# A graph layer with gathers and one-hot products: more nodes by slots, fewer by chunks, a pause between gathers, and x theta^T computed beside B

## The chip, the core and the metric

The kernel runs on one core of a Trainium2 chip. The metric is the device time of one execution in microseconds; given is the median of ten runs.

## The reference

`x` is 6250 x 256; `src` and `dst` hold 100000 edges, sorted by `dst`. Cut to what matters:

```python
e = relu((x[dst] - x[src]) @ theta_w.T + theta_b + x[src] @ phi_w.T + phi_b)
out = segment_max(e, dst, num_segments=6250)
out = where(isfinite(out), out, 0.0)
return layernorm(x + out, axis=-1, eps=1e-5)
```

What depends on the destination is the same for all edges into a node, and relu doesn't change an order. So the kernel computes, for each node, `relu(max over its edges of B[src] + x theta^T)`, where `B = x (phi - theta)^T + biases` has one row for each source.

## The kernel before, in words

**B.** x is loaded in pieces of four rows per partition, transposed on TensorE (L669), copied by ACT (L671), multiplied by the weights (L675, two products of 128x256 for each 128 rows), and DVE adds the bias (L678). The pieces `b_sb` are stored to the tensor `b_rows` in HBM.

**Part 1, the chunks.** The first N1 = 6250 - 128*TILES nodes have the first edges of the sorted list. These edges are cut into 128 chunks of FIRST_STEPS columns, one chunk per partition. GpSimd gathers a column of 128 rows of `b_rows` by an indirect DMA (`gather`, L467 to 469), eight columns into one tile `g` of the pool `gathered` (RING tiles of 1 MB); DVE keeps the running maximum along the chunk, reset by `caps` at the border of a node (`run`, L717 to 726, the instruction at L722); SP writes the group to `maxima_1` in HBM. X_GROUPS of the even groups are gathered from x itself, before B is there, and multiplied on the chip (L696 to 699). `node_place` (L762), `places_1`, `chunk_heads`, `tails_1` (L811) and `heads_1` find the last edge of each node and carry a maximum over the borders of chunks.

**Part 2, the slots.** The last 128*TILES nodes lie TILES to a partition. From `dst_w`, a window of WINDOW edges per partition, ACT counts where each node's edges begin (L628, a sum of signs), eight counts in a batch; then a gather brings up to R = 36 sources of each node (`table_i`, L475). `sources` (L853 to 874) turns source numbers into a slot and a row; a slot is 375 rows of B, in KB = 3 blocks of 125. `choice` (L877) picks, two slots at a time, at most one edge of each node in each slot, and takes it out of what is left; `wanted` (L912) stores the choice to `chosen_rows`. `slot_part` (L939) brings the chosen rows of one slot for 1024 nodes, builds their one-hot (L949 on DVE, one block; L951 and L952 on ACT, two), multiplies it by the slot's rows of B in two terms (24 products, L959), and DVE keeps the maximum in `acc` (L970). With 17 slots and 4 chunks of nodes these are 68 parts. What wasn't chosen goes to a list (`list_pieces`, L980 to 1042) of LIST columns, gathered and reduced as part 1's chunks are (`group_2`, L1044), into `maxima_2`.

**End.** `rows_of` (L1051) loads x for a share of tiles, gathers their maxima, multiplies x by theta^T (L1071 to 1079), for part 2 transposes `acc` (L1086) and takes the larger, adds, and applies relu (L1087 to 1091). `normalise` (L1096) makes the layer norm on ACT and DVE (squares L1104, L1111) and stores the rows. The shares of part 1 lie among the list's groups, those of part 2 stand behind the last part.

**What sets the order.** Pieces are emitted as L1127 to 1177 say: `sources`; nine choice steps with two chunk groups behind each; the list's pieces; the remaining chunk groups with PACE slot parts per group; then the list's groups with PACE parts per group; what remains of the parts; the end. From that a scheduler makes one fixed order for each engine. Every engine takes its instructions in that order, an instruction that waits holds up all behind it.

Of the kernel before, what the change touches and what calls it, by code (L numbers as in the profile page):

```python
# [48 lines left out]
P = 128  # L49
# [3 lines left out]
RING = 7  # L53
GENERAL_STEPS = 17
FIRST_STEPS = 275
X_GROUPS = 5
X_BEFORE = 2
TILES = 32
LIST = 240
WINDOW = 640  # L60
# [5 lines left out]
PACE = 1.2  # L66
# [339 lines left out]
def gnn_kernel(ctx: ExitStack, tc: tile.TileContext, x, src, dst, theta_w, theta_b, phi_w, phi_b, out):  # L406
# [4 lines left out]
    Q = N // P  # L411
    LEFT = N - P * Q
    NT = Q + 1
    XQ = 4
# [8 lines left out]
    NB = N // ROWS  # L423
    NS = -(-NB // KB)
# [4 lines left out]
    assert D == 2 * P and LEFT > 0 and LEFT1 > 0 and Q % XQ == 0 and OWN % CW == 0  # L429
    assert (P - 1) * T + 1 < E <= P * T and N < ID_MASK and P * T <= EDGES and E + 8 * P <= EDGES  # L430
    assert N == NB * ROWS and SLOT * NS < ABSENT and KB * P <= SLOT and WINDOW <= 8 * P and P * T1 < E
    assert LIST % STEPS == 0 and TILES <= 32

# [4 lines left out]

    b_rows = dram.tile([N, D], FP, name="b_rows")
# [5 lines left out]

    x_main = x[: P * Q, :].rearrange("(p q) d -> p q d", q=Q)
    b_main = b_rows[: P * Q, :].rearrange("(p q) d -> p q d", q=Q)
    b_block = b_rows.rearrange("(b r) d -> r b d", r=ROWS)


    x_1 = x[: P * Q1, :].rearrange("(p q) d -> p q d", q=Q1)
    x_2 = x[N1:, :].rearrange("(p q) d -> p q d", q=TILES)
    out_1 = out[: P * Q1, :].rearrange("(p q) d -> p q d", q=Q1)
    out_2 = out[N1:, :].rearrange("(p q) d -> p q d", q=TILES)
    maxima_1t = maxima_1[: P * T1, :].rearrange("(p t) d -> p t d", t=T1)
    maxima_2t = maxima_2[: P * LIST, :].rearrange("(p t) d -> p t d", t=LIST)

    def iota(t, step, base, per_partition):
        nc.gpsimd.iota(
            t,  # L460
            pattern=[[step, t.shape[1]]],
            base=base,
            channel_multiplier=per_partition,
            allow_small_or_imprecise_dtypes=True,
        )

    def gather(to, table, offsets):  # L467
        nc.gpsimd.indirect_dma_start(  # L468
            out=to, out_offset=None, in_=table, in_offset=bass.IndirectOffsetOnAxis(ap=offsets, axis=0)
        )  # L470

    def gather_run(to, table, offsets):

        n = to.shape[1]
        nc.gpsimd.indirect_dma_start(  # L475
            out=to,
            out_offset=None,
            in_=flat(table, 0, [[n, EDGES // n], [1, n]]),
            in_offset=bass.IndirectOffsetOnAxis(ap=offsets, axis=1),
        )  # L480
# [15 lines left out]

    for i in of_x[:X_BEFORE]:
        gather_group(i, x)
# [28 lines left out]

    weights = const.tile([P, 2, KC, D], FP, name="weights")
    bias = const.tile([P, 1, D], FP, name="bias")

# [13 lines left out]
    with (  # L544
        tc.tile_pool(name="sort", bufs=1) as sort,
        tc.tile_pool(name="ps_sort", bufs=2, space=PSUM) as ps_sort,
    ):
        n_unsorted = nc.values_load(flags[0:1, 0:1])
        with tc.If(n_unsorted > 0):
            sort_edges(nc, sort, ps_sort, src, dst, src_list, dst_list, ident)  # L550
            load_chunks(nc.sync, dst_i, dst_list, T, EDGES)
            load_chunks(nc.sync, dst_1, dst_list, T1, EDGES)
            load_rows(nc.scalar, src_1, src_list, P * T1)
            for i in of_x[:X_BEFORE]:
                gather_group(i, x)
# [51 lines left out]
    accs = body.enter_context(tc.tile_pool(name="accs", bufs=1))  # L607
    acc = accs.tile([P, KC, OWN], FP, name="acc")
    index = body.enter_context(tc.tile_pool(name="index", bufs=1))
    dst_w = index.tile([P, WINDOW], I32, name="dst_w")  # L610
    gather_run(dst_w, dst_list, edge0_i)
    for i in of_x[X_BEFORE:]:
# [10 lines left out]
    BATCH = 8  # L623
    for j0 in range(0, TILES + 1, BATCH):
        j1 = min(j0 + BATCH, TILES + 1)
        for j in range(j0, j1):
            junk = index.tile([P, WINDOW], BF, name="junk")
            nc.scalar.activation(  # L628
                junk, local, AF.Sign, bias=halves[:, j : j + 1], scale=-1.0, accum_out=sums[:, j : j + 1]
            )  # L630
        nc.vector.tensor_scalar(begin[:, j0:j1], sums[:, j0:j1], 0.5, 0.5 * WINDOW, op0=ALU.mult, op1=ALU.add)
# [8 lines left out]

    with (
        tc.tile_pool(name="prep", bufs=1) as prep,
        tc.tile_pool(name="x_in", bufs=3) as x_in,
        tc.tile_pool(name="b_out", bufs=2) as b_out,
        tc.tile_pool(name="ps_t", bufs=3, space=PSUM) as ps_t,
        tc.tile_pool(name="ps_b", bufs=3, space=PSUM) as ps_b,
    ):
        w_in = prep.tile([P, 2, KC, D], FP, name="w_in")
        for i, w in enumerate((theta_w, phi_w)):
            nc.sync.dma_start(w_in[:, i], w.rearrange("(c p) k -> p c k", p=P))  # L650
        biases = prep.tile([P, 2, D], FP, name="biases")
        for i, b in enumerate((theta_b, phi_b)):
            nc.sync.dma_start(biases[:, i, :], flat(b, 0, [[0, P], [1, D]]))
        nc.vector.tensor_add(bias[:, 0, :], biases[:, 0, :], biases[:, 1, :])
        nc.vector.tensor_sub(w_in[:, 1], w_in[:, 1], w_in[:, 0])
        for i in (1, 0):
            for c in range(KC):
# [3 lines left out]
                nc.vector.tensor_copy(weights[:, i, :, c * P : (c + 1) * P], ps[:, 0])  # L661

        def b_of(to, rows):

            n = rows.shape[1]
            ps = ps_t.tile([P, 2, KC, P], FP, name="ps_xt")
            for i in range(n):
                for k in range(KC):
                    nc.tensor.transpose(ps[:, i, k, :], rows[:, i, k * P : (k + 1) * P], ident)  # L669
            x_t = prep.tile([P, 2, KC, P], FP, name="x_t", bufs=3)  # L670
            nc.scalar.copy(x_t[:, :n], ps[:, :n])  # L671
            ps = ps_b.tile([P, 2, D], FP, name="ps_b")
            for i in range(n):
                for k in range(KC):
                    nc.tensor.matmul(  # L675
                        ps[:, i, :], x_t[:, i, k, :], weights[:, 1, k, :], start=(k == 0), stop=(k == KC - 1)
                    )
            nc.vector.tensor_tensor(to, ps[:, :n, :], bias.to_broadcast([P, n, D]), op=ALU.add)  # L678

        for q in range(0, NT, XQ):  # L680
            n = min(XQ, NT - q)
            b_sb = b_out.tile([P, XQ, D], FP, name="b_sb")
            x_q = x_in.tile([P, XQ, D], FP, name="x_q")
            if q < Q:
                nc.sync.dma_start(x_q, x_main[:, q : q + XQ, :])
            else:
                nc.vector.memset(x_q[:, 0, :], 0.0)
                nc.sync.dma_start(x_q[:LEFT, 0, :], x[P * Q :, :])
            for i in range(0, n, 2):
                w = min(2, n - i)  # L690
                b_of(b_sb[:, i : i + w, :], x_q[:, i : i + w, :])
            if q < Q:
                nc.scalar.dma_start(b_main[:, q : q + XQ, :], b_sb)
            else:
                nc.scalar.dma_start(b_rows[P * Q :, :], b_sb[:LEFT, 0, :])
        for i in of_x:  # L696
            for k in range(0, STEPS, 2):
                rows = ring_tiles[i][:, k : k + 2, :]
                b_of(rows, rows)
# [14 lines left out]
    ps_fetch = fetch.enter_context(tc.tile_pool(name="ps_fetch", bufs=3, space=PSUM))  # L714
    last = {1: None, 2: None}
# [120 lines left out]

    def table(name, dtype=FP):
# [7 lines left out]
    BATCH_S = 2  # L845

# [6 lines left out]
    def sources():  # L853
        nc.vector.tensor_copy(source.rearrange(by_rank, r=R), table_i.rearrange("p j r -> p r j"))
        floor_of(work_1, source, ROWS)
        floor_of(work_2, work_1, KB)
        nc.vector.scalar_tensor_tensor(source, work_1, float(P - ROWS), source, op0=ALU.mult, op1=ALU.add)
        nc.vector.scalar_tensor_tensor(source, work_2, float(SLOT - KB * P), source, op0=ALU.mult, op1=ALU.add)
        nc.gpsimd.iota(
            rank.rearrange(by_rank, r=R),  # L860
            pattern=[[1, R], [0, TILES]],
            base=0,
            channel_multiplier=0,
            allow_small_or_imprecise_dtypes=True,
        )
# [6 lines left out]
        nc.vector.scalar_tensor_tensor(work_1, source, float(-ABSENT), work_2, op0=ALU.add, op1=ALU.mult)  # L872
        nc.vector.tensor_scalar(padded, work_1, float(ABSENT), None, op0=ALU.add)
        nc.vector.memset(unused, 1)


    def choice(s0):  # L877
# [17 lines left out]
        at = index.tile([P, BATCH_S, 1, TILES], I16, name="at")  # L895
        for i in range(n):
            blocks = min(KB, NB - (s0 + i) * KB)
            nc.vector.tensor_scalar(
                at[:, i, 0, :], low[:, i, :W], (blocks - 1) * P + ROWS, None, op0=ALU.min
            )  # L900
        nc.vector.tensor_copy(chosen[:, s0 : s0 + n, :], at[:, :n, 0, :])
# [24 lines left out]
    def slot_terms(s):  # L926

        blocks = min(KB, NB - s * KB)
        f = raw
        even = ROWS // 16 * 16  # L930
        nc.sync.dma_start(f[:even, :blocks, :], b_block[:even, s * KB : s * KB + blocks, :])
        nc.sync.dma_start(f[even:ROWS, :blocks, :], b_block[even:, s * KB : s * KB + blocks, :])
        terms = terms_of[s] = slots.tile([P, PARTS, KB, D], FR, name="terms")
        nc.scalar.copy(terms[:, 0, :blocks], f[:, :blocks])
        nc.vector.tensor_tensor(
            terms[:, 1, :blocks], f[:, :blocks], terms[:, 0, :blocks].bitcast(FP), op=ALU.subtract
        )

    def slot_part(s, c):  # L939
        if c == 0:  # L940
            slot_terms(s)
        blocks = min(KB, NB - s * KB)
# [4 lines left out]
        for b in range(blocks):  # L947
# [5 lines left out]
        for h in range(KC):  # L953
            ps = ps_fetch.tile([P, CW], FP, name="ps_f")
            n = blocks * PARTS
# [23 lines left out]

# [246 lines left out]
```

## Time and profile before

| | |
|---|---|
| median of 10 runs | 907.36 us (902.37 to 912.56) |
| the profiled execution | 914.0 us |
| its span in the trace | 912.2 us |
| mean granted TensorE clock | 0.854 |
| first gather of the tables (POOL) | 63.76 us |
| last gather of the tables ends | 104.0 us |
| first gather from `b_rows` | 123.94 us |
| last running maximum of the list ends | 830.7 us |
| first gather of the end | 836.6 us |

PE is TensorE's products, PEld its weight loads, DVE VectorE, ACT ScalarE, POOL GpSimd, SP the engine that issues most loads and stores. In a line of the costliest groups stand the line of the kernel, the engine, the operation, what it writes and reads with the shape, and how often; behind the first bar the busy time and the mean in ns; behind the second the engine's idle time just before these instructions, and what ended most of it. In a timeline line stand the start, the duration, and in brackets the idle time before it. "Issue" as a releaser is time in which an engine waited for nothing that the profile shows. The slices cut the span in 40 equal pieces, with the busy share in tenths.

### The profile page before, as it was taken

What the parts mean: (1) busy time and instruction counts of PE and PEld (TensorE: products, weight loads), DVE (VectorE), ACT (ScalarE), POOL (GpSimd) and SP (SyncE); (2) the same over time, 40 slices, a digit from 0 to 9 for tenths busy, and PEclk for the clock granted to TensorE, in tenths of its full rate; (3) what the DMA queues carried; (4) which work ended last, traced back from release to release, by engine and by line L of the source; (5) the groups of instructions that cost most, each with busy time, mean ns of one, the idle gap of its engine ahead of it and who ended that gap; (6) DMA issues with size and microseconds to landing.
All of it is one profiled execution on the core that took longest, in us unless ns stands there. A gap on an engine that the chain in (4) does not pass through costs nothing. (4 is left out here: it accounts for less than half of the span.)

```text
span 912.2 us, 9291 instructions
## 1 busy us (share of the span) xinstructions
PE 610.9 (67%) x2557; PEld 483.6 (53%) x2557; DVE 632.7 (69%) x1309; ACT 429.0 (47%) x680; POOL 652.8 (72%) x622
## 2 busy tenths in 40 slices
PE   0459799576402655979406795857979898874782
PEld 0248688465301544768304574646868677653661
DVE  2223599999978776778309784846979787793764
ACT  0159232557201333467603555355967757420575
POOL 6767457788888877777777477777777777774730
PEclk9979899878755777889856899878999999898897
DMA  7366346776644657777537798666888788867342
GB/s 250 111 191 220 118 162 205 252 255 218 224 143 143 207 182 246 234 234 265 169 104 241 262 295 272 208 193 230 277 279 268 236 279 256 282 220 276 101 160 108
DMA packets 63082, 195.61 MB, mean 214 GB/s; under 512 B 14071, under 2 KB 22795, under 8 KB 53515
## 3 DMA queue, kind: packets, MB, share of 16 engines
q1 hardware_dynamic: 32207, 112.01, 34.2%
q0 software_dynamic: 28272, 75.14, 28.4%
q10 hardware_dynamic: 2540, 7.75, 2.4%
q8 instruction: 23, 0.38, 0.2%
q14 instruction: 40, 0.33, 0.1%
HBM read 114.27 MB, written 81.38 MB: 214 GB/s over the span
## 5 line engine op out<-in xcount | busy, mean ns | idle before, releaser
L959 PE MATMUL ps_f<-hot,terms 128*128 128x512 f32 x1600 | 417.2, 421 | 175.8 <-DVE hot L949 127.7
L959 PEld LDWEIGHTS ps_f<-hot,terms 128*128 128x128 f32 x1600 | 322.3, 205 | 260.6 <-issue 124.7
L722 DVE SCALAR_TENSOR_TENSOR g<-g,caps 128x256 f32<-128x256 f32 x513 | 246.3, 482 | 147.3 <-DMA g<-b_rows,list_src 100.7
L468 POOL DMA_INDIRECT g<-b_rows,src x235 | 280.7, 1194 | 75.3 <-issue 65.9
L468 POOL DMA_INDIRECT g<-b_rows,list_src x240 | 246.3, 1026 | 73.1 <-issue 63.7
L951 ACT ACTIVATE hot<-want,minus_row 128x1024 fp32r<-128x1024 f16 x132 | 146.0, 1144 | 165.1 <-PE ps_f L959 145.8
L970 DVE TENSOR_TENSOR acc<-acc,ps_f 128x1024 f32<-128x1024 f32 x128 | 155.6, 1216 | 4.7 <-PE ps_f L959 4.3
L952 ACT ACTIVATE hot<-hot 128x1024 fp32r<-128x1024 f32 x132 | 133.8, 1049 | 0.4
L675 PE MATMUL ps_b<-weights,x_t 128*128 128x256 f32 x356 | 86.7, 400 | 20.7 <-ACT x_t L671 19.9
L675 PEld LDWEIGHTS ps_b<-weights,x_t 128*128 128x128 f32 x356 | 69.0, 199 | 34.3 <-ACT x_t L671 25.0
L468 POOL DMA_INDIRECT g<-maxima,place x49 | 47.7, 973 | 41.2 <-issue 20.8
L949 DVE TENSOR_SCALAR hot<-want,row_id 128x1024 fp32r<-128x1024 f16 x68 | 51.9, 763 | 2.2 <-ACT hot L952 1.2
L468 POOL DMA_INDIRECT g<-in_x_dram,src x40 | 38.7, 967 | 15.9 <-issue 11.3
L671 ACT COPY x_t<-ps_xt 128x512 f32<-128x512 f32 (+1 forms) x45 | 24.7, 577 | 50.8 <-PE ps_xt L669 31.3
L1077 PE MATMUL ps_e<-weights,x_t 128*128 128x256 f32 x128 | 34.9, 418 | 18.9 <-ACT x_t L1073 18.9
L475 POOL DMA_INDIRECT table_i<-src_list,begin_i x32 | 30.2, 944 | 13.9 <-issue 8.8
L1077 PEld LDWEIGHTS ps_e<-weights,x_t 128*128 128x128 f32 x128 | 24.5, 202 | 26.4 <-ACT x_t L1073 23.4
L771 ACT ACTIVATE junk<-ps,upper 128x275 bf16<-128x275 f32 x34 | 16.2, 482 | 45.4 <-PE ps L768 45.3
L678 DVE TENSOR_TENSOR b_sb<-ps_b,bias 128x512 f32<-128x512 f32 (+1 forms) x25 | 16.9, 679 | 26.5 <-PE ps_b L675 26.5
L628 ACT ACTIVATE junk<-local,halves 128x640 bf16<-128x640 f32 x33 | 27.4, 830 | 16.4 <-DVE local L615 13.2
L1077 PE MATMUL ps<-weights,x_t 128*128 128x256 f32 x68 | 20.5, 453 | 18.8 <-ACT x_t L1073 13.6
L1104 ACT ACTIVATE squares<-g,r 128x256 bf16<-128x256 f32 x49 | 24.3, 498 | 14.4 <-DVE r L1101 12.5
(194 smaller groups left out, 489.3 us busy)
## 6 DMA issues: line engine op xcount, KB each, us to landing
maxima<-g SPq DMA_DIRECT2D x64, 1024.0 KB
want<-chosen_rows SPq DMA_DIRECT2D x68, 256.0 KB
x_q<-in_x_dram SPq DMA_DIRECT2D x12, 512.0 KB
b_rows<-b_sb ACTq DMA_DIRECT2D x12, 512.0 KB
raw<-b_rows SPq DMA_DIRECT2D x16, 336.0 KB
g<-in_x_dram SPq DMA_DIRECT2D x5, 1024.0 KB
out_dram<-g SPq DMA_DIRECT2D x5, 1024.0 KB
g<-b_rows,list_src POOLq DMA_INDIRECT x240, 4.5
```

The lines of the kernel that those rows point to most:

```text
L468: nc.gpsimd.indirect_dma_start(out=to, out_offset=None, in_=table, in_offset=bass.IndirectOffsetOnAxis(ap=offsets, axis=0))
L475: nc.gpsimd.indirect_dma_start(out=to, out_offset=None, in_=flat(table, 0, [[n, EDGES // n], [1, n]]), in_offset=bass.IndirectOffsetOnAxis ...
L628: nc.scalar.activation(junk, local, AF.Sign, bias=halves[:, j : j + 1], scale=-1.0, accum_out=sums[:, j : j + 1])
L671: nc.scalar.copy(x_t[:, :n], ps[:, :n])
L675: nc.tensor.matmul(ps[:, i, :], x_t[:, i, k, :], weights[:, 1, k, :], start=(k == 0), stop=(k == KC - 1))
L722: nc.vector.scalar_tensor_tensor(g[:, k, :], last[part], caps[:, t : t + 1], g[:, k, :], op0=ALU.min, op1=ALU.max)
L949: nc.vector.tensor_scalar(hot[:, b, :], want, row_id[:, b : b + 1], None, op0=ALU.is_equal)
L951: nc.scalar.activation(hot[:, b, :], want, AF.Abs, bias=minus_row[:, b : b + 1], scale=1.0)
L952: nc.scalar.activation(hot[:, b, :], hot[:, b, :].bitcast(FP), AF.Relu, bias=1.0, scale=-1.0)
L959: nc.tensor.matmul(ps[:, w : w + 512], terms[:, part, b, h * P : (h + 1) * P], hot[:, b, w : w + 512], start=(i == 0), stop=(i == n - 1),)
L970: nc.vector.tensor_tensor(to, to, ps, op=ALU.max)
L1077: nc.tensor.matmul(a[:, i, :], x_t[:, 2 * i + c, :], weights[:, 0, c, :], start=(c == 0), stop=(c == KC - 1))
```

## The change

- TILES goes from 32 to 40, so part 2 has 5120 nodes instead of 4096, part 1 1130 instead of 2154; FIRST_STEPS goes from 275 to 146, LIST from 240 to 288, WINDOW from 640 to 800, PACE from 1.2 to 2.2. There are five chunks of nodes, so 85 parts.
- Three groups instead of five are gathered from x, eight gathers ahead of the branch, eight behind it and eight behind `dst_w`.
- The ring has four tiles; a second pool `ring_2` of seven, opened where the tables of the choice are closed, serves the list and the end.
- Every indirect gather is followed by an iota into a tile `pause` of 128x144, which nothing reads; fixed dependencies put gather, iota, gather in one order.
- x theta^T is computed with B (one product 512 wide for each half of x's columns), copied by ACT to `a_sb`, stored to `a_rows` in HBM, and loaded in `rows_of`; the end has no transposes of x and no products.
- Counts come in batches of ten, six by ACT and four by DVE.
- A slot's rows are dealt to its blocks in turn (row KB*p + b instead of blocks of 125); `sources` changes with it.
- One chunk group instead of two behind each choice step, a slot part behind every other one; parts are then paced by the list alone.
- The shares of the end have eight tiles each, and max and add are done on four tiles at once instead of two.

```diff
-RING = 7
-FIRST_STEPS = 275
-X_GROUPS = 5
-TILES = 32
-LIST = 240
-WINDOW = 640
-PACE = 1.2
+RING = 4
+RING_2 = 7
+FIRST_STEPS = 146
+X_GROUPS = 3
+TILES = 40
+LIST = 288
+WINDOW = 800
+PACE = 2.2
+PAUSE = 144
...
+    def indirect(out, in_, in_offset):
+        in_turn = mybir.DependencyInfo(mybir.DependencyClass.NoSync, mybir.DependencyReason.DATA)
+        one = nc.gpsimd.indirect_dma_start(out=out, out_offset=None, in_=in_, in_offset=in_offset)
+        if after_gather[0] is not None:
+            tc.add_manual_dep(one.ins, after_gather[0], in_turn, reason="a break between gathers")
+        count = iota(pause, 1, 0, 0)
+        tc.add_manual_dep(count.ins, one.ins.name, in_turn, reason="a break between gathers")
+        after_gather[0] = count.ins.name
...
-    for i in of_x[:X_BEFORE]:
-        gather_group(i, x)
+    gather_group(of_x[0], x)
...
-    BATCH = 8
+    BATCH, BY_SIGNS = 10, 6
...
+            else:
+                nc.vector.tensor_scalar(
+                    junk, local, halves[:, j : j + 1], None, op0=ALU.is_le, op1=ALU.add, accum_out=begin[:, j : j + 1]
+                )
...
+        weights = prep.tile([P, KC, 2, D], FP, name="weights")
...
+        for share in shares(4):
...
+            for i in range(0, n, 2):
+                w = min(2, n - i)
+                x_t = x_transposed(x_q[:, i : i + w, :])
+                ps = ps_b.tile([P, 2, 2, D], FP, name="ps_b")
+                for h in range(w):
+                    for k in range(KC):
+                        nc.tensor.matmul(
+                            ps[:, h], x_t[:, h, k, :], weights[:, k], start=(k == 0), stop=(k == KC - 1)
+                        )
+                add_bias(b_sb[:, i : i + w, :], ps[:, :w, 0, :])
+                nc.scalar.copy(a_sb[:, i : i + w, :], ps[:, :w, 1, :])
+            nc.scalar.dma_start(node_rows(b_rows, *share), present(b_sb, *share))
+            nc.scalar.dma_start(node_rows(a_rows, *share), present(a_sb, *share))
...
     def group_2(t0):
-        g = gathered.tile([P, STEPS, D], FP, name="g")
+        g = ring_2.tile([P, STEPS, D], FP, name="g")
...
+        x_f = ring_2.tile([P, STEPS, D], FP, name="g")
+        a = ring_2.tile([P, STEPS, D], FP, name="g")
...
+        nc.sync.dma_start(present(x_f, *share), node_rows(x, *share))
+        nc.sync.dma_start(present(a, *share), node_rows(a_rows, *share))
+        m = ring_2.tile([P, STEPS, D], FP, name="g")
...
-        for k in range(0, n, 2):
-            w = min(2, n - k)
-            ps = ps_tile().rearrange("p (i n) -> p i n", i=4)
-            for i in range(w):
-                for c in range(KC):
-                    nc.tensor.transpose(ps[:, 2 * i + c, :], x_f[:, k + i, c * P : (c + 1) * P], ident)
...
+        for k in range(0, n, 4):
+            w = min(4, n - k)
+            some = m[:, k : k + w, :]
...
-            nc.vector.tensor_tensor(two, two, a[:, :w, :], op=ALU.add)
+            nc.vector.tensor_tensor(some, some, a[:, k : k + w, :], op=ALU.add)
...
     sources()
     for s0 in range(0, NS, BATCH_S):
         choice(s0)
         wanted(s0)
-        for _ in range(2):
-            group_1(groups_1.pop(0))
-        if s0 == 0:
+        some_groups_1(1)
+        if s0 % 4 == 0:
             fetch_parts(1)
...
+    tables.close()
+    ring_2 = body.enter_context(tc.tile_pool(name="ring_2", bufs=RING_2, side="right"))
+    some_groups_1(len(groups_1))
...
+    for t0 in range(0, LIST, STEPS):
+        group_2(t0)
         pace += PACE
         while pace >= 1.0:
             fetch_parts(1)
             pace -= 1.0
```

## The prediction

> **What bounds the kernel now.** I read the busy shares first, then the slices, the costliest groups, the waits, and last GpSimd's own timeline.
>
> ```profile
> PE 610.9 (67%) x2557; PEld 483.6 (53%) x2557; DVE 632.7 (69%) x1309; ACT 429.0 (47%) x680; POOL 652.8 (72%) x622
> POOL 6767457788888877777777477777777777774730
> L959 PE MATMUL ps_f<-hot,terms 128*128 128x512 f32 x1600 | 417.2, 421 | 175.8 <-DVE hot L949 127.7
> L722 DVE SCALAR_TENSOR_TENSOR g<-g,caps 128x256 f32<-128x256 f32 x513 | 246.3, 482 | 147.3 <-DMA g<-b_rows,list_src 100.7
> L468 POOL DMA_INDIRECT g<-b_rows,src x235 | 280.7, 1194 | 75.3 <-issue 65.9
> L468 POOL DMA_INDIRECT g<-b_rows,list_src x240 | 246.3, 1026 | 73.1 <-issue 63.7
> ```
>
> No engine is full, but POOL's slices never fall below 4 until the last two, and the idle time in front of its gathers is "issue": it waits for nothing. The waits say so outright:
>
> ```profile
> POOL g L468 <- issue: 161.6, 492, 8.3
> ```
>
> and its timeline shows what the "issue" is:
>
> ```profile
> 57.70 0.95 POOL L468 DMA_INDIRECT g<-in_x_dram,src  x1 [0.30 <-issue]
> 58.65 1.29 POOL L859 IOTA rank<- 128x1152 f32 x1
> ...
> 103.10 0.94 POOL L475 DMA_INDIRECT table_i<-src_list,begin_i  x1 [0.30 <-issue]
> 104.04 0.36 POOL L459 IOTA local<- 128x240 f32 x1
> ```
>
> A gather has 0.30 ahead of it wherever gathers follow each other; so the undisturbed period is 0.946+0.305=1.25 us. The 599 gathers average 1.079+0.305. From 124 us (first gather from b_rows) to 828 us (end of the list) POOL does little else, so **POOL's gathers are the bound**; after 837 the end is a chain through POOL, DVE, ACT and the store. Gathers without a DVE operation beside them take 0.95; those beside a busy DVE 1.2 to 1.4 on the mean between 124 and 350 us, one of them 4.29 (at 263.9).
>
> **The change, part by part.** Counts after it are from the static order of each engine. All sums are against the profiled execution (span 912.2, time 914.0); this is 6.6 above the median 907.36.
>
> *Tables.* x gathers 40→24, table gathers 32→40. Gather dst_w stood behind 17 x gathers issued after the branch (27.50) and began at 48.84; 8 in front of it now, 9x1.25 less: 37.5, which edge0 (ready at 36.5) allows. From it to the first table gather lay 14.9 (63.76-48.84), with eight sign counts at 0.83 in it; six counts at 0.83x800/640 come out near the same, 12 to 13 since the first batch waits for fewer. So the first table gather comes at 49.5 and the last ends 40x1.252=50 later: 99.5 (before 104.0). The table lands at 101 (before 105.47).
>
> *B, and x theta^T beside it.* This is the loss that I am surest of. Before, 19 of the 25 bias adds (L678) came ahead of the first source operation, which waits for the table; the last, at 118.5, let the gathers start at 123.94. After, PE's product is 512 wide instead of 256, ACT copies the other half, and only 6 adds stand ahead of that wait; the other 19 lie among the source and choice operations, the last one behind the ninth choice step. So DVE must do all this after 101: the sources, 10.6 us before without the adds, times 40/32 nodes and 12 passes for 10, 15.6; 8.5 choice steps at 5.1 (start to start) times 40/32=6.3, 54; 19 adds at 0.6, 11.4; in all 81. PE's 17 to 19 pairs beside it need about 4.1 each (eight 512-wide products at twice the 0.227 us of a 256-wide one, and four transposes), 70 to 78: covered, but barely; without this cover nothing more is lost, since the longer of the two counts. With 5 us for store and start (123.94-118.54), b_rows is ready at **187**, 63 later than before. ACT's copies hide (3.60 busy in 19 us between 105 and 124).
>
> *Chunks.* 235 gathers from b_rows become 122. Two periods bound theirs: 1.25 undisturbed, 1.2 to 1.4+0.3=1.5 to 1.7 beside the choice. The choice is over by then, the list's making is not: 1.40, near to the 350-to-470 stage (120/92=1.30). 122x1.40=171. The ring falls from 7 to 4 tiles, three of which hold x groups, so groups 3 and 5 wait for groups 0 and 2 to be written behind the choice: 17 us. End of the chunks 187+171+17=375 (before 471: 96 us won back and more).
>
> *List.* 240 gathers become 288, with 9 of maxima and 2 for heads and scatter between: 299 periods of 1.315 (what 1.01 to 1.02+0.30 makes): 393, to 768; the last running max 2.5 later, 770.5 (before 830.7).
>
> *The pauses.* After each gather an iota of 128x144 is put in fixed order, so all 461 gathers on this path (40+122+299) carry one. No row shows an iota and a gather both unblocked. Bounds: the iota starts at the gather's end (58.65, 104.04) and could run in the 0.305 that is empty anyway: 0. Or it is added in full: between a 128x128 at 0.21 to 0.25 and a 128x240 at 0.36, so 0.25x461=+115. Below nothing: a break could at most take away the stretch by DVE, 0.15x122+0.063x299=-37. I take 0: the rows nearest to it show that an iota starts with no gap, that a gather starts 0.27 after what releases it, so that the 0.30 looks like the gather's own start, which the queue can do beside an iota.
>
> *Slots.* 68 parts become 85, 24 products each: 2040x0.235=480 us of PE (24x0.235=5.64 at granted clock 0.97, up to 6.26 lower). DVE gets 17x3.4 and ACT 17x4.4 us more, both under PE. In DVE's order 12 parts' one-hots and 27 of the 160 acc operations still stand behind the list's last running max; before, acc was done 7 us ahead of it. That **tail** has no gathers left to lie beside: 12.5 parts at 5.7 to 5.8, 72 us. What POOL wins at the list is paid here. acc done at 843.
>
> *End.* No x transposes, no theta products (128 at 418 ns there), but a load of x theta^T per share on SP, under the gathers of maxima. Five shares of eight: DVE 2x1.22 (max), 2x1.22 (add), 8x0.48, about 2.5 for the root: 11.2 each, 56; behind the last, ACT's 8x(0.50+0.5) and the store, 15; waits for ring tiles in shares 3 to 5, 4: **75** (before 81.5 behind the last running max). Span 918.
>
> A page of the Trainium skill speaks against the iotas. "SBUF — State Buffer", section "Who interferes with whom", says that DVE and GpSimd share one port pair by an exclusive lock and that the loser waits for the whole instruction; the trace agrees with its sense (0.95 alone, 4.29 at worst), though our stretch also stands beside running maxima with two SBUF inputs, which the page leaves out for descriptor writing. By it, an iota would be one more holder of the lock, 0.25 us at a time, and the sum would move up by as much as some 100 us if every one met DVE. "Perfetto Trace Analysis", section "GPSIMD Engine Instruction", says to time that engine by start-to-start spacing; by that rule the 0.30 may be part of the gather itself, with nothing to hide in, and the sum would be that of the first rival. I keep zero.
>
> **Sum.** 101+86+188+393+2.5+72+75 = 918 of span, 920 for such an execution, less 6.6: **913 us**, +0.6%. Its own range, with ±15 on the b_rows start, ±12 on the chunk period and ±10 on the end, is 885 to 940.
>
> **Rivals.**
> A. *The iota is additive.* For it: POOL is strictly in order, and the 0.30 may be fixed after each instruction. 0.21x461=+97: 1010; half hidden, 960. Decides from 0.05 us visible on.
> B. *Faster: the breaks and the quiet start take away the stretch.* Gathers fall to 0.946 everywhere, 37 us less, and with POOL idle during the choice DVE's steps shorten by some 8: 913-45=868; half of it 890. For it: undisturbed stages at 0.95; against it: in the list the stretch is only 0.063, and nothing says that an iota keeps DVE off a gather. It decides from 0.02 us per gather on.
> C. *The change doesn't shorten the chunks as it says*: the 122 gathers meet the list's making and the one-hots of the early parts at 1.6 instead of 1.40: +24, 937. For it: the mean of 200 to 350 us.
>
> **How the numbers follow.** My case 0.45, A 0.20, B 0.25, C 0.10. About 0.3% (2.7 us) is what a measurement can tell from no change. Of my case three tenths lie faster and an eighth within: faster 0.25+0.135=0.38, same 0.08, slower 0.54. The range takes all of B and my case, C, and A up to nine tenths of the iota visible: 866 to 1000.
>
> **What would show it.** First gather from b_rows near 187 (wrong, if near 130); spacing of list gathers 1.31 (A: 1.52; B: 1.25); last list running max near 770; PE busy without a break for 72 us behind it; 75 us from last acc to the end. If that tail is short, the sum is 30 to 60 too high; if the spacing is over 1.4, it is too low.

## The result, and the profile after

The changed kernel takes 1026.7 us in the median (1022.85 to 1032.59, nine runs), the kernel before 908.0 beside it: a ratio of 1.1313, 95% interval 1.1285 to 1.1341. That is 119 us slower, beyond the upper end of the forecast's range. The profiled execution's span is 1025.2. Here and below a ratio and its interval take only the executions within 1.5% of the fastest of their kernel (where one alone is left, no interval is given), a median takes all of them.

From the page of the changed kernel, the busy shares, the slices of POOL and the groups that answer to those shown before:

```profile
PE 671.1 (65%) x2607; PEld 497.0 (48%) x2607; DVE 688.5 (67%) x1233; ACT 488.2 (48%) x690; POOL 722.9 (71%) x1073
...
POOL 6688300178988888888888888888888886710560
...
L992 PE MATMUL ps_f<-hot,terms 128*128 128x512 f32 x2040 | 510.8, 411 | 136.8 <-DVE hot L982 114.9
...
L479 POOL DMA_INDIRECT g<-b_rows,list_src x288 | 298.8, 1038 | 47.8 <-issue 45.8
L750 DVE SCALAR_TENSOR_TENSOR g<-g,caps 128x256 f32<-128x256 f32 x432 | 205.9, 481 | 146.2 <-DMA g<-b_rows,list_src 103.5
...
L479 POOL DMA_INDIRECT g<-b_rows,src x122 | 151.4, 1241 | 104.2 <-DMA b_rows<-b_sb 76.3
...
L465 POOL IOTA pause<- 128x144 f32 x524 | 151.0, 288 | 3.4
```

Three things are new. POOL has a hole in slices 5 to 8 (from 107 to 202 us), and the group of chunk gathers names what ended it: 76.3 us on the store of B. What makes the store late is DVE's order: from the first source operation at 109.0 to the last bias add at 198.7 DVE was nearly always busy, and its 19 adds in that stretch waited 1.1 us for PE in all. Of DVE's groups from 109 to 199:

```profile
L693 DVE TENSOR_TENSOR b_sb<-ps_b,bias 128x512 f32<-128x512 f32 x19 | 13.0, 684 | 1.1 <-PE ps_b L709 1.1
```

Behind the hole POOL is fuller than before, but 151 us of its work are iotas, which bring nothing. And in slices 36 and 37 POOL has another hole. It lies beside this piece of the chain that ended last (start, duration, what):

```profile
868.08 72.60 PE ps_f L992 x312
```

72.6 us of products without a break, behind the end of the list. The timeline of GpSimd shows what a gather and its iota cost:

```profile
52.16 0.95 POOL L479 DMA_INDIRECT table_i<-src_list,begin_i  x1 [6.79 <-DVE begin_i L646]
53.11 0.28 POOL L465 IOTA pause<- 128x144 f32 x1
53.55 0.95 POOL L479 DMA_INDIRECT table_i<-src_list,begin_i  x1 [0.16 <-issue]
54.51 0.28 POOL L465 IOTA pause<- 128x144 f32 x1
54.94 0.96 POOL L479 DMA_INDIRECT table_i<-src_list,begin_i  x1 [0.16 <-issue]
```

The iota starts where the gather ends. But then 0.16 us pass before the next gather, not zero, and not the 0.305 of before. From gather to gather the median is 1.396 (about 0.96 for the gather, 0.01, 0.27 for the iota, 0.16), against 1.252.

Cut at the marks that the prediction used, its terms stand beside two traces: the changed kernel, and the same without iotas (e1, below). All in us of span.

| stage | predicted | changed | without iotas |
|---|---|---|---|
| tables landed | 101 | 109.0 | 101.5 |
| to the first gather from b_rows | 86 | 93.1 | 98.0 |
| chunk gathers, to the first of the list | 188 | 214.9 | 201.0 |
| list, to its last gather's end | 393 | 448.7 | 401.8 |
| to the last running max | 2.5 | 5.8 | 5.7 |
| to the last maximum into acc | 72 | 70.5 | 67.8 |
| to the end | 75 | 83.3 | 90.4 |
| span | 918 | 1025.2 | 966.2 |

### The profile page after: what moved, and what is told of

Its sections match the earlier page's. It is cut to its first block, busy times and chain, and to the rows that moved or that the text cites. A ratio compares the mean times of both kernels' runs of the same rounds, so it can differ in the third digit from the quotient of the medians.

```text
span 1025.2 us, 9698 instructions
## 1 busy us (share of the span) xinstructions
PE 671.1 (65%) x2607; PEld 497.0 (48%) x2607; DVE 688.5 (67%) x1233; ACT 488.2 (48%) x690; POOL 722.9 (71%) x1073
## 4 chain that ended last, share of the span: by engine, by line
POOL 47%; DVE 16%; PE 13%; issue 11%; DMA 7%; ACT 4%; POOLq 0%; DVEq 0%; SPq 0%; ACTq 0%
POOL g L479 33%; POOL pause L465 10%; PE ps_f L992 9%; POOL table_i L479 4%; PE ps_b L709 3%; DVE g L750 3%; DMA g<-b_rows,list_src 3%; ACT g L1130 2%; DVE acc L1003 1%; DVE junk_v L642 1%; DMA g<-maxima,place 1%; DMA want<-chosen_rows 1%; DVE lowest L919 1%; DVE b_sb L693 1%; DMA g<-b_rows,src 1%
## 5 line engine op out<-in xcount | busy, mean ns | idle before, releaser
L992 PE MATMUL ps_f<-hot,terms 128*128 128x512 f32 x2040 | 510.8, 411 | 136.8 <-DVE hot L982 114.9
L992 PEld LDWEIGHTS ps_f<-hot,terms 128*128 128x128 f32 x2040 | 402.7, 200 | 242.6 <-issue 115.8
L479 POOL DMA_INDIRECT g<-b_rows,list_src x288 | 298.8, 1038 | 47.8 <-issue 45.8
L750 DVE SCALAR_TENSOR_TENSOR g<-g,caps 128x256 f32<-128x256 f32 x432 | 205.9, 481 | 146.2 <-DMA g<-b_rows,list_src 103.5
L984 ACT ACTIVATE hot<-want,minus_row 128x1024 fp32r<-128x1024 f16 x170 | 186.9, 1145 | 238.1 <-PE ps_f L992 214.0
L479 POOL DMA_INDIRECT g<-b_rows,src x122 | 151.4, 1241 | 104.2 <-DMA b_rows<-b_sb 76.3
L1003 DVE TENSOR_TENSOR acc<-acc,ps_f 128x1024 f32<-128x1024 f32 x160 | 194.4, 1215 | 27.7 <-PE ps_f L992 27.7
L985 ACT ACTIVATE hot<-hot 128x1024 fp32r<-128x1024 f32 x170 | 169.8, 1045 | 0.0
L465 POOL IOTA pause<- 128x144 f32 x524 | 151.0, 288 | 3.4
L709 PE MATMUL ps_b<-weights,x_t 128*128 128x512 f32 x196 | 95.1, 641 | 60.5 <-ACT x_t L689 48.6
```

The lines of the kernel that those rows point to most:

```text
L465: return nc.gpsimd.iota(t, pattern=[[step, t.shape[1]]], base=base, channel_multiplier=per_partition, allow_small_or_imprecise_dtypes=True,)
L479: one = nc.gpsimd.indirect_dma_start(out=out, out_offset=None, in_=in_, in_offset=in_offset)
L709: nc.tensor.matmul(ps[:, h], x_t[:, h, k, :], weights[:, k], start=(k == 0), stop=(k == KC - 1))
L750: nc.vector.scalar_tensor_tensor(g[:, k, :], last[part], caps[:, t : t + 1], g[:, k, :], op0=ALU.min, op1=ALU.max)
L984: nc.scalar.activation(hot[:, b, :], want, AF.Abs, bias=minus_row[:, b : b + 1], scale=1.0)
L985: nc.scalar.activation(hot[:, b, :], hot[:, b, :].bitcast(FP), AF.Relu, bias=1.0, scale=-1.0)
```

## The experiments

**e1, the iotas taken away.** The fixed order of the gathers stays.

```diff
-        count = iota(pause, 1, 0, 0)
-        tc.add_manual_dep(count.ins, one.ins.name, in_turn, reason="a break between gathers")
-        after_gather[0] = count.ins.name
+        after_gather[0] = one.ins.name
```

> The changed kernel without the iota behind each gather; the fixed order of the gathers stays. Theory (each iota costs 0.14 us of POOL, 1.396 against 1.252 from gather to gather, on 461 gathers ahead of the end): 66 less, 945 to 970; list gathers 1.37 apart on the mean (1.517 now), first gather from b_rows at 195 to 198 instead of 202. Rival (another wait, DVE's or PE's, takes the place of the iota): over 1000, with idle time of POOL ahead of list gathers.

968.3, ratio to the kernel before 1.0639 (1.0589 to 1.0689): 58 less than with iotas. The period of undisturbed gathers is back at 1.252. The theory holds within 8 us; what is missing lies in the end, which got 7 longer (83.3 to 90.4), and in the making of B, which got 5 longer: with the table 7.5 earlier, DVE's adds waited 4.5 for PE instead of 1.1. Some 60 us of loss are left, and no iota is in them.

**e2, the iotas put into the kernel before.** `indirect` of the change is called by `gather` and `gather_run` of the kernel before; nothing else is changed.

> The kernel before with the same iota of 128x144 behind each indirect gather and the same fixed order, nothing else changed. Theory: 0.14 on 539 gathers (32 of tables, 235, 240 and 32): +77, 975 to 995. Rival (the iota itself is cheap, the loss lies in the rest of the change): 908 to 930.

999.6 against 909.2 beside it (1.0968, 1.0918 to 1.1018): 90 more. Some 77 are the iotas, at 0.144. What the rest is can be seen in part. In the new order 24 of the 40 x gathers, instead of 7, stand between the gather of dst_w and the first table gather; that one comes at 75.65 instead of 63.76, and the last table gather ends at 119.85 instead of 104.04, where 32 iotas explain 4.6. So iotas cost much the same in a kernel that has none of the other edits.

**e3, iotas of one element.**

```diff
-PAUSE = 144
+PAUSE = 1
```

> The changed kernel with iotas of one element instead of 144. Theory (gather to gather = 0.95 + 0.01 + the iota's length + 0.16, so that an iota of about 0.14 just fills what was 0.305 before): spacing 1.25 to 1.27, time within 10 of the kernel without iotas, 950 to 970. Rival (each further instruction costs a fixed 0.14): spacing 1.39, 1020 to 1030.

983.8 (1.0794, 1.0745 to 1.0843). The timeline of GpSimd with one element:

```profile
55.58 0.15 POOL L465 IOTA pause<- 128x1 f32 x1
55.88 0.95 POOL L479 DMA_INDIRECT table_i<-src_list,begin_i  x1 [0.16 <-issue]
56.84 0.15 POOL L465 IOTA pause<- 128x1 f32 x1
57.15 0.95 POOL L479 DMA_INDIRECT table_i<-src_list,begin_i  x1 [0.16 <-issue]
```

The same place without any iota (e1):

```profile
55.41 0.94 POOL L479 DMA_INDIRECT table_i<-src_list,begin_i  x1 [0.30 <-DMA table_i<-src_list,begin_i]
56.66 0.94 POOL L479 DMA_INDIRECT table_i<-src_list,begin_i  x1 [0.30 <-issue]
```

1.271 against 1.252 and 1.396. The 0.16 stays whatever the iota's length, so of the 0.305 between gathers 0.145 can be filled with another instruction, and the rest can't. An iota of 144 elements fills the 0.145 and stands out by as much again; one of a single element stands out by 0.02. The rival (a fixed price per instruction) is out. The time is 15.5 above e1's, 14 over the upper end expected; 461x0.02 = 9 of it is the period. In the trace the excess lies in the list (9.9) and the chunks (5.8): the list's gathers last 1.046 on the mean against 1.019 in e1, the chunks' 1.259 against 1.230, and the iotas 0.187 where an undisturbed one takes 0.15. What lengthens them isn't shown.

**e4, the bias adds put ahead of the sources**, iotas kept.

```diff
+            one = nc.vector.tensor_tensor(to, ps, bias.to_broadcast([P, ps.shape[1], D]), op=ALU.add)
+            adds.append(one.ins.name)
...
+        tc.add_manual_dep(first.ins, adds[24], in_turn, reason="the adds first")
```

> The changed kernel, iotas kept, with the first operation of the sources put behind all 25 bias adds in DVE's order. Theory (the 19 adds among the choice steps delay b_rows): first gather from b_rows at 130 to 140 instead of 202; the chunk gathers then lie beside the choice and stretch, so 30 to 60 of the 65 reach the end, 965 to 995. Rival (the choice step behind them, now later, or the ring of four, holds the chunks up as long): over 1010.

1034.4 (1.1369, 1.1314 to 1.1423), 8 more than the changed kernel. The first gather from b_rows came at 162.9, not at 135. DVE's timeline shows why; in brackets is what it waited for:

```profile
95.68 0.69 DVE L694 TENSOR_TENSOR b_sb<-ps_b,bias 128x512 f32<-128x512 f32 x1 [4.90 <-PE ps_b L711]
99.12 0.69 DVE L694 TENSOR_TENSOR b_sb<-ps_b,bias 128x512 f32<-128x512 f32 x1 [2.74 <-PE ps_b L711]
104.71 0.69 DVE L694 TENSOR_TENSOR b_sb<-ps_b,bias 128x512 f32<-128x512 f32 x1 [4.90 <-PE ps_b L711]
```

Two adds in 9.03 us: with the adds first PE is what they wait for; with products 512 wide it gives one every 4.5, and the last comes at 158.8. So the first gather from b_rows came 39 earlier than in the changed kernel (202.0): DVE's order had held it up by that much, of the 62 to 72 that the theory named, and PE holds it up from there. But the time didn't follow. The sources begin 50 us later here (159.4 instead of 109.0), and the choice steps and the slot parts that need them lie later too. Against the 39 gained, the chunk gathers, now beside the choice, take 24 more, the list 6 and the tail 14. The theory's place for the delay is right; its forecast of the time fell.

**e5 and e6, x theta^T left out of the making of B**, both without iotas; e6 also with e4's order. The products are 256 wide again, and `a_rows` gets the rows of B: this part of the result is another.

```diff
-                            ps[:, h], x_t[:, h, k, :], weights[:, k], start=(k == 0), stop=(k == KC - 1)
+                            ps[:, h, 0, :], x_t[:, h, k, :], weights[:, k, 0, :], start=(k == 0), stop=(k == KC - 1)
```

> No iotas, and x theta^T left out of the making of B (the products are 256 wide again; the rows stored to a_rows are those of B, so the output is another): what the second half of the product costs. In DVE's order 8 adds instead of 6 stand ahead of the sources and the last one behind 7 of the choice operations on the leftover mask instead of 10. Theory (DVE's order holds b_rows up, with x theta^T second): first gather from b_rows at 165 to 180 (199.5 with it), time 940 to 955 against 968. Rival (the wider product alone held it up): below 150, under 930.

> The same without iotas and without x theta^T, and all adds ahead of the sources. Theory (with the 512-wide product an add came every 4.6 us on the mean, too slow to end ahead of the table; with 256 it comes every 2.6 or so): adds done near 105, first gather from b_rows at 110 to 120, the chunk gathers beside the choice at 1.6 to 1.7 apart, 895 to 925. Rival (PE's tail behind the list sets the end, so that an earlier start only makes the tail longer): over 940.

960.6 (1.0596, 1.0557 to 1.0635) and 954.3 (1.0503, 1.046 to 1.0545), against 968.3 of e1. (e5 to e8 ran on another chip, where the kernel before took 906.9 instead of 909.2.) The first gather from b_rows came at 180.7 and at 131.9 instead of 199.5. So both the order and the wider product make B late: the narrow product alone brings it 19 earlier (e5), the order alone 39 (e4, with iotas), both together 68; in e6 adds come every 2.8. e5's theory missed by less than 1 in the start and by 6 in the time; e6's missed in both. For 68 us of earlier start became 14 us of time. The chunk gathers lie beside the choice again (1.44 us each on the mean instead of 1.23) and take back 26 of the 68, the list 13, and the tail of PE, which grew from 68 to 86, takes 18. So e6's rival has the time right, but the longer tail is less than half of its reason.

**e7, 32 nodes per partition in the changed kernel**, without iotas.

```diff
-FIRST_STEPS = 146
-TILES = 40
-LIST = 288
-WINDOW = 800
-PACE = 2.2
+FIRST_STEPS = 275
+TILES = 32
+LIST = 240
+WINDOW = 640
+PACE = 1.2
```

> The changed kernel without iotas, and with TILES 32, FIRST_STEPS 275, LIST 240, WINDOW 640, PACE 1.2 as before: what 40 nodes per partition bring. No one-hot stands behind the list's last running max in DVE's order, so no tail of PE. Theory (late start 195 to 200, then 251 gathers from b_rows at 1.5, 240 and 20 at 1.32, end 85): 985 to 1020, slower than with 40 tiles (968). Rival (the tail of 68 costs more than the fewer gathers bring): below 960.

971.6 (1.0701, 1.0658 to 1.0745), as long as with 40. With 32 the last running max comes at 880.5 instead of 808.0, but acc is done at 816, ahead of it. So 40 nodes win 72 us on POOL, and 68 of these are given back in the tail. Neither theory nor rival: the gain of POOL and the price of PE cancel. Set beside the kernel before, which has 32 nodes too, e7 shows what a late B costs where no tail stands behind the list: its first gather from b_rows comes 61 later (185.1 against 123.9), its last running max 50 later (880.5 against 830.7). The two differ in more than that, so the 50 are not the late start's alone.

**e8, 40 nodes per partition in the kernel before.** A ring of 5 is what fits.

```diff
-RING = 7
-FIRST_STEPS = 275
-X_GROUPS = 5
-TILES = 32
-LIST = 240
-WINDOW = 640
-PACE = 1.2
+RING = 5
+FIRST_STEPS = 146
+X_GROUPS = 3
+TILES = 40
+LIST = 288
+WINDOW = 800
+PACE = 2.2
...
-        for _ in range(2):
-            group_1(groups_1.pop(0))
+        group_1(groups_1.pop(0))
```

> The kernel before with TILES 40, FIRST_STEPS 146, LIST 288, WINDOW 800, PACE 2.2, X_GROUPS 3, and a ring of 5 (no more room), one chunk group behind each choice step; no iotas, x theta^T at the end as before. 25 adds of 25 stand ahead of the sources, 7 one-hots behind the list's last running max. Theory (40 nodes are a gain, and what follows the table's landing late made the loss): first gather from b_rows at 115 to 130, list ends near 740, tail 40 to 50, end 90: 860 to 895. Rival (the tail and the smaller ring eat it): over 915.

883.75, ratio 0.9767 (0.9714 to 0.9819): **shorter than both kernels**, by 23 and 143 us. The first gather from b_rows comes at 113.4, the last running max at 747.95, acc is done at 783.4. Set its list beside that of e1. Stages: span, then busy time of PE, PEld, DVE, ACT, POOL with instruction counts, granted clock, DMA share, GB/s. e8, list and tail:

```profile
334.00:743.00 409.00, 367.93 (x1556) 294.48 (x1555) 338.92 (x567) 280.43 (x340) 305.23 (x299) 0.96 0.79 253
743.00:783.00 40.00, 39.24 (x175) 32.13 (x173) 30.95 (x34) 21.95 (x21) 16.24 (x17) 1.00 0.57 187
```

e1, list and tail:

```profile
400.00:802.00 402.00, 324.63 (x1355) 261.27 (x1356) 318.14 (x528) 247.02 (x266) 304.30 (x300) 0.90 0.79 255
802.00:876.00 74.00, 72.59 (x322) 59.80 (x321) 45.70 (x47) 49.82 (x49) 15.89 (x17) 1.00 0.41 136
```

POOL does the same in both lists. PE does 368 us in the one and 325 in the other; 33 of the 43 that it lacks in e1 are the longer tail (72.6 against 39.2), where POOL has nothing left to do beside them. e8 emits a slot part with every piece of the list's making and PACE with each remaining chunk group; the change paces parts by the list alone, and emits a part with every fourth piece.

**e9 to e18, parts where they were before, and more pace for e8.** e9, e13 and e17 are one kernel: e1 with

```diff
-        if i % 4 == 0:
-            fetch_parts(1)
+        fetch_parts(1)
...
-    some_groups_1(len(groups_1))
+    pace = 0.0
+    while groups_1:
+        some_groups_1(1)
+        pace += PACE
+        while pace >= 1.0:
+            fetch_parts(1)
+            pace -= 1.0
```

e10 and e14 have the same edit on e6, e11 and e15 are e8 with PACE 3.6, e12 and e16 with PACE 5, and e18 is e1 again, on e17's chip.

> The changed kernel without iotas, and with the slot parts emitted as before the change: one with every list piece, and PACE of them with each remaining chunk group, not with the list alone. In DVE's order 1 one-hot instead of 11 stands behind the list's last running max. Theory (the parts' place makes the tail of 68): tail 5 to 20, list end at most 20 later, 915 to 940 against 968. Rival (PE can't do the parts earlier, the wait only moves into the list): over 955.

> The same with x theta^T left out of the making of B (another output) and all adds ahead of the sources: three causes taken away, the iotas, the late b_rows, the late parts. Theory (these three are the whole loss; the earlier start alone had brought only 6 because the tail stood behind it): 880 to 905, near the 883.75 of the kernel before with 40 nodes. Rival (something else in the change, the ring of four or the end, costs as well): over 920.

> The kernel before with 40 nodes per partition (883.75), PACE 3.6 instead of 2.2: 4 one-hots instead of 7 behind the list's last running max. Theory (the tail of 35 there is paid in full): tail 20 to 25, 868 to 880. Rival (running maxima now wait behind PE's parts, the ring of 5 stops the gathers): 884 or more.

> The same with PACE 5: no one-hot and no maximum into acc behind the list's last running max. Theory: tail gone, the list's end 10 to 20 later, 862 to 880. Rival (the list is then held up by PE as long as the tail was): 884 or more, with idle time of POOL on DVE's running maxima.

> The changed kernel without iotas and with the slot parts emitted as before the change (one with every list piece, PACE of them with each remaining chunk group), on a chip where the kernel before takes its 907. Theory (the parts' place makes the tail of 68): tail 5 to 20 behind the list's last running max, the list's end at most 20 later, 915 to 940 against 968. Rival (PE can't do the parts earlier, the wait only moves into the list): over 955.

> The same with x theta^T left out of the making of B (another output) and all adds ahead of the sources. Theory (iotas, late b_rows and late parts are the whole loss): 880 to 905, near 883.75. Rival (something else in the change, the ring of four or the end, costs as well): over 920.

> The kernel before with 40 nodes per partition and PACE 3.6 instead of 2.2 (883.75). Theory (the tail of 35 there is paid in full): tail 20 to 25, 868 to 880. Rival (running maxima wait behind PE's parts and hold up the ring of 5): 884 or more.

> The same with PACE 5: nothing of the parts behind the list's last running max. Theory: tail gone, list end 10 to 20 later, 862 to 880. Rival (the list is held up by PE as long as the tail was): 884 or more, with POOL idle on DVE's running maxima.

> The changed kernel without iotas and with the slot parts emitted as before the change (one with every list piece, PACE of them with each remaining chunk group). Theory (the parts' place makes the tail of 68): against the changed kernel without iotas beside it, 28 to 53 less, a tail of 5 to 20 behind the list's last running max, the list's end at most 20 later. Rival (PE can't do the parts earlier, the wait only moves into the list): within 13 of it.

> The changed kernel without iotas again, for the comparison with the one before it on the same chip: 968 where the kernel before takes 907, tail 68.

In these ten the kernel before took 1130 to 1134 us, on three chips, one of which had run e1 to e4 at 909; so their times stand only beside each other and not beside e1 to e8. e18 is the program of e1, and PE's idle time ahead of the slots' products is 233 in it against 97. These lines are of e1, then of e18:

```profile
L990 PE MATMUL ps_f<-hot,terms 128*128 128x512 f32 x2040 | 497.7, 405 | 96.5 <-DVE hot L980 61.1
...
L990 PE MATMUL ps_f<-hot,terms 128*128 128x512 f32 x2040 | 540.2, 426 | 232.9 <-issue 83.6
L982 ACT ACTIVATE hot<-want,minus_row 128x1024 fp32r<-128x1024 f16 x170 | 187.2, 1147 | 403.6 <-remote 245.3
L1001 DVE TENSOR_TENSOR acc<-acc,ps_f 128x1024 f32<-128x1024 f32 x160 | 194.5, 1217 | 243.1 <-remote 180.0
```

"Remote" is a releaser that the profile finds nowhere on this core. Within e18's list PE gets some products one by one:

```profile
705.83 0.40 PE L990 MATMUL ps_f<-hot,terms 128*128 128x512 f32 x1 [1.24 <-issue]
707.92 0.59 PE L990 MATMUL ps_f<-hot,terms 128*128 128x512 f32 x1 [1.70 <-issue]
709.33 0.79 PE L990 MATMUL ps_f<-hot,terms 128*128 128x512 f32 x1 [0.82 <-issue]
```

The profile shows no cause for this; that stays open. The numbers expected of e9 to e16 are therefore untested.

| kernel | median | kernel before beside it | ratio (interval) |
|---|---|---|---|
| e9 | 1121.1 | 1134.0 | 0.9951 (0.9893 to 1.0009) |
| e10 | 1112.3 | 1134.0 | 0.9832 (0.9762 to 0.9903) |
| e11 | 1092.8 | 1134.0 | 0.9627 (0.9492 to 0.9763) |
| e12 | 1097.9 | 1134.0 | no interval |
| e13 | 1114.4 | 1130.7 | no interval |
| e14 | 1098.7 | 1130.7 | 0.9759 (0.9641 to 0.9877) |
| e15 | 1059.1 | 1130.7 | 0.9419 (0.9331 to 0.9506) |
| e16 | 1049.8 | 1130.7 | 0.9361 (0.9245 to 0.9477) |
| e17 | 1109.6 | 1129.7 | 0.9728 (0.9613 to 0.9843) |
| e18 | 1138.1 | 1129.7 | no interval |

What can be compared directly is the pair on one chip, e17 against e18. The medians of four executions each are 28.5 apart; those that a ratio would take are 1105.1 and 1089.3 against a single 1117.8, 21 apart. That lies between the theory (28 to 53) and the rival (within 13), so the time doesn't decide. The traces do show the tail: it goes from 75 us (971.7 to 1046.9) to 12 (1009.2 to 1021.2). Of the 63, 37 are given back by a later end of the list, and 18 are left in the span. So the parts' place does make the tail, but less than half of the tail was gained by moving them. And 40 nodes in the kernel before, with PACE 3.6 or 5, stay faster than it in these runs as well. Whether 3.6 or 5 is better than 2.2 isn't told, since e8 itself didn't run there.

## Why the prediction was wrong

What bounds each stage was mostly seen; the likeliest case was chosen wrongly, and several terms were too small. Against 918 the span was 1025.2, 107 more: 59 are the iotas (e1's span against the changed kernel's), 48 are in e1 too. Of these 48, 12 lie in the making of B, 13 in the chunks, 9 in the list, 3 up to the last running max and 15 in the end; the tail was 4 shorter.

- **The pauses**: the step that failed. The prediction took 0, between 0 and 0.25, because "a gather starts 0.27 after what releases it, so that the 0.30 looks like the gather's own start, which the queue can do beside an iota". Half of this is so: 0.145 of the 0.305 runs beside the iota, 0.16 doesn't (e3). An iota of 0.27 then costs 0.144, on 461 gathers 66, measured 58. Without it the time is 968.3, inside the stated range. Rival A had the sign and the place; its "half hidden, 960" was the right price on a sum that was too low elsewhere. Its reason, a fixed 0.30 after each instruction, was not right either.
- **"Below nothing", the gathers' stretch**: the iotas took none of it away. The list gathers last 1.038 us on the mean with iotas and 1.019 without, the chunk gathers 1.241 and 1.230. Rival B has nothing left.
- **Tables**: 101, and 101.5 in e1, which is luck: the gather of dst_w began at 31.6 there instead of 37.5, and the first table gather came 18.8 behind it instead of 12 to 13. Of the 7.5 more in the changed kernel 6 are the iotas between the table gathers (40x0.144).
- **B late**: 202.0, predicted 187. The reason was right: DVE's work between the table's landing and the last add set it, and PE's products, if at 4.5 an add instead of 4.1, were covered but for 1.1 us. 8 of the 15 are the table's later landing; and DVE took 90 instead of 81, most of that in the choice (some 61 instead of 54). But the loss does not reach the end in full: bringing b_rows 39 us (e4) or 68 us (e6) earlier changed the time by +8 and -14, because the chunk gathers beside the choice, the list and the tail take back most of it. In e8, whose b_rows and parts are both early, the list ends 60 us earlier than in e1 and the tail is 32 shorter; that the two go together there is argued, not shown.
- **Chunks**: 188, measured 214.9 with iotas and 201.0 without. The ring's waits were right (17 expected, 14.5 found in e1), the period of 1.40 too small: (201-14.5)/122 = 1.53. Rival C, where the gathers meet the list's making, had the direction; its 1.6 is somewhat over.
- **List**: 393 at 1.315; e1 has 401.8, with 300 gathers and some waits between them. With the iotas, 448.7.
- **Tail**: 72 predicted, 70.5 found, 72.6 of products in one piece. It came from counting, in DVE's order, the one-hots behind the last running max. This step was right. How much of it can be had back isn't settled (e17, e18).
- **End**: 75, measured 83.3 and in e1 90.4. The last three shares wait for ring tiles, 4 us expected. Behind acc's end at 941.9 these waits come to 8.9, 6.7 and 1.6, in all 17; the first of them began beside the tail:

```profile
950.84 0.96 POOL L479 DMA_INDIRECT g<-maxima,place  x1 [49.92 <-DVE g L1112]
968.87 0.97 POOL L479 DMA_INDIRECT g<-maxima,place  x1 [6.73 <-DVE r L1126]
```

L1112 is DVE's relu in `rows_of`, here the last one of the first share, which sets a ring tile free. So shares 3 to 5 are gathered one after another, the last ending at 992.6. Without x transposes and theta products the end, counted from acc's last maximum, is not short: 83.3 for 40 tiles, 94.8 in e8 for 40 with them, 88.4 before for 32.

On the page "SBUF — State Buffer" of the Trainium skill ("Who interferes with whom"): the runs don't show iotas and DVE blocking each other by much. 21 of 524 iotas take over 0.35 us, the running maxima last 481 ns with iotas and 480 without, and e1's gathers are as long as the changed kernel's within 0.02. What an iota costs is its length less what fits in the gap.
The rule of "Perfetto Trace Analysis" (section "GPSIMD Engine Instruction"), to time GpSimd from start to start, was the right one to follow: 1.252, 1.271 and 1.396 give the price of each iota, and the zero was read off spans and gaps.

What stays open: how the 85 us between e8 and e1 divide into x theta^T with B and the adds' order, the parts' place, the ring, and the end. e6 gives 14 for the first two while the parts' place stands, e17 against e18 gives 21 to 28 for that one in those later runs; they were taken away together only there (e10, e14), and the ring was not tested.

## What to carry to other kernels

A gap that is the same after every instruction of an engine need not be free room: measure from start to start with a filler of two lengths before it is counted as cover. When work is moved from the bound engine to one that has slack on the average, look in the fixed order for how much of it stands behind the last instruction of the bound engine: here 68 of 72 us won were paid there (e7), and 18 of the 68 us of an earlier start went into it (e6). And work moved ahead of a point that everything waits for (x theta^T ahead of B) delays that point: without it b_rows came 19 us earlier here, and the time was some 8 shorter (e5).

## What the runs showed of the hardware that was not expected

An instruction between two indirect gathers is overlapped in part: 0.145 of 0.305 us, by iotas of 0.15 and of 0.27 alike. fp32 products of 128x512 last 0.641 us on the mean in the records, those of 128x256 0.400, so the wider product is not twice the time in the records; a pair of adds, where it waited for PE, took 9.0 us with it (e4) and 5.6 without (e6).
